# Reordering the plan in front of the first scan: port marks, weight casts and bias rows in a conv-attention hybrid kernel

## The chip, the cores and the metric

The kernel runs on one core of one Trainium2 chip. The metric is the device time of one execution in microseconds, the median of several runs. A core has five engines with queues of their own: PE (TensorE, matrix products into PSUM), DVE (VectorE), ACT (ScalarE), POOL (GpSimd) and SP (SyncE, which here only issues DMAs). Each engine takes its instructions strictly in the order in which the program emitted them. An instruction waits on semaphores for its data only; where two engines share no data, nothing on the chip ties them in time.

## The reference, cut to what matters

Two layers run over `x` of shape (4, 64, 64, 96). Only the beginning of the first bears on the change:

```python
x = x + _L0_conv_ref(_gn(x), ...)      # _gn: group norm, 32 groups of 3 channels, over a whole image
# in _L0_conv_ref:
xn = (x - mu) * rsqrt(var + 1e-3) * ln_gamma + ln_beta       # layer norm over the 96 channels
proj = xn.reshape(B, L, C) @ W_in + b_in                     # L = 4096, 96 -> 3*96 + 3*96*16
# proj is cut into value u, gate, delta d and A, B, C (16 states for each channel)
h_new = d * (A_t * h) + d * (B_t * u_t)                      # a scan along L
y = gate * sum(C_t * h_new, axis=states)
...
# second layer: linear attention, then a feed-forward net in quantised fp8, each with a residual
```

So before the first scan step can run, the group norm of the first image (a mean and a variance over all 4096 positions), the layer norm of the first 512 positions, the transposition and the projections with `W_in` must be done, one after another.

## The kernel before, in words

**Tiling.** Each image of 4096 positions is cut into 8 chunks of 512. For a chunk the scan runs over 12 tiles (`Tile`, L901): 4 groups of states (`sh`) by 3 groups of 32 channels (`cg`), each 128 partitions by 512 positions. There are 384 tiles in all. A tile is three projections on PE (B, A, C, each of three matmuls, L294), ACT's copy of B out of PSUM (`b_copy`, L926), POOL's multiply (`b_mul`, L929), DVE's multiply of A (`a_mul`, L938), the scan on DVE (L945) and a multiply by C (`c_mul`, L969). From the seventh tile (`START = 6`, L1399) on, the main loop (L1588) emits these in a fixed pattern; everything else is hung on steps of that loop.

**Precision.** The projections work in fp32r with a high and a low part. For each weight block ACT casts the high part (`high`, L326), then DVE or POOL subtracts to get the low part (`split_low`, L284), then two SP DMAs build a third, mixed block (`split_copies`, L286 to L288). The blocks are `w_dug` (for d, u and gate), `w_rep` (columns of `w_dug` repeated four times over, written by `repeat`, L316, on ACT; `n = 0` is the high part, `n = 1` the low) and twelve blocks `w_bac[k]` for k = B, A, C and `sh` = 0 to 3. The low parts of `sh` 0 and 1 are DVE's, those of 2 and 3 POOL's. The raw weights come in by SP DMAs at the start, B's first, then A's, then C's.

**The start.** `planned_start` (L1403) lists what has to be done up to the seventh tile as jobs with an engine, a cost, predecessors and a rank. The class `Plan` (L489) is a list scheduler: it takes again and again the job that can start first by its own clock; among jobs within 0.3 us of each other it takes the lower rank, then the longer tail (the cost of all that hangs on the job). Jobs `land(...)` are no instructions: they stand for a time before which something isn't expected. A job marked `port=True` on DVE isn't placed before the last marked job on POOL has ended, and the other way round. The result is only an **order of emission** on each engine; the planner's times do not exist on the chip. Where PE would idle in the plan, filler matmuls (`stay_awake`, L1535) are emitted.

The chain it places first, with the lines of the trace: group norm statistics (L644), aggregate (L647), group means (`m`: L685, L693 to L701), group variances (`r`: L685, L705, and the root on POOL, L708); for each of the two a diagonal on ACT (L719), a `spread` on PE (L725) and `spread_out` on ACT (L734); then for the first chunk `centre` (L780), `scale` (L783), layer norm statistics (L432 to L439), the root on POOL (`rstd`, L410), the apply on DVE (`apply_vector`, L480), transposes (L800), `affine` (L804), `upper` (L808), `low_in_place` (L839, three instructions), the wide products for d and u (L844), `wide_d` on ACT (L849), `wide_du` on DVE (L856), and then the tiles. Beside it lie: `high_dug` and `low_dug`, `repeat`, the bias rows (`bias_rows`, L336 and L340, on DVE; `bias_turn`, L348 and L351, on PE; `bias_out`, L355 and L356, on DVE), the weight casts, and the second chunk's front (`second`: `centre` and `scale` on POOL, statistics on DVE, root on POOL, apply on ACT, transposes, `low`, L813, with three SP DMAs, L814 to L816, and its own d and u). Late weights are loaded by SP in one job (`load_late`, L266).

Of the kernel before, what the change touches and what calls it, by code (L numbers as in the profile page):

```python
# [75 lines left out]
GN_FIRST = (10, 14, 21, 26, 34, 41, 46, 54)  # L76
GN_CHAIN = (0, 0, 1, 2, 6, 6, 8, 8, 8, 9, 11, 11)
XBUFS = 15
END_TRIES = 250
END_SEED = 25  # L80

# [2 lines left out]
def conv_attn_hybrid_kernel(  # L84
# [19 lines left out]
    nc = tc.nc  # L104
# [1298 lines left out]
    def planned_start():  # L1403
        plan = Plan({"A": 2, "B": 1, "C": 1, "D": 1, "M": 3, "bu": 5, "h": 3})
        plan.LOOK = 0.3
        job = plan.job
        plan.rank = -5

        def land(what, time):
            return job(what, time, lambda: None)  # L1410

        def mm(cost, fn, *args, after, key):
            return job("PE", cost, fn, *args, after=after, take=[key])

        q, first, second = GroupNorm(0), Front(0, 0), Front(0, 1)
        x = [land(f"x{n}", 3.6 + 0.8 * n) for n in range(NCH)]
        raw = [land(f"raw{n}", t) for n, t in enumerate((15.8, 19.8, 24.0))]
        a = []
        for n in range(NCH):
            key = f"{'AM'[n % 2]}:g{n}"  # L1420
            t = mm(0.5, q.turn, n, "AM"[n % 2], after=[x[n]], key=key)
            a = [job("DVE", 0.85, q.stats, n, after=[t, *a], free=[key])]
        b = job("DVE", 0.8, bias_rows, after=[x[3]])
        b = mm(0.8, bias_turn, after=[b], key="M:b")
        b = job("DVE", 0.35, bias_out, after=[b], free=["M:b"])
        a = job("DVE", 0.4, q.aggregate, after=a)
        m = job("DVE", 1.1, q.all_of, ("group_sums", "m"), ("mean",), ("squares",), after=[a])
        r = job("DVE", 0.7, q.all_of, ("group_sums", "v"), ("offset",), ("root",), after=[m], late=0.9)
        g = []
        for n, a in enumerate((m, r)):  # L1430
            a = job("ACT", 0.37, q.diagonal, n, n + 1, after=[a, *g])
            a = mm(0.75, q.spread, n, n + 1, after=[a], key=f"M:s{n}")
            g = [job("ACT", 0.25, q.spread_out, n, n + 1, after=[a], free=[f"M:s{n}"])]
            if n == 0:
                c = job("DVE", 0.56, first.centre, nc.vector, after=g)


        calm = land("calm", 22)
        hd = job("ACT", 0.43, high_dug, after=[land("raw", 11.9)])
        ld = job("POOL", 0.8, low_dug, after=[hd])  # L1440
        wd = job("SP", 1.0, split_copies, w_dug[:, 0], w_dug[:, 1], w_dug[:, 2], after=[ld], late=2.2)
        wr = [job("ACT", 0.45, repeat, n, k, after=[(hd, ld)[n]]) for n in range(2) for k in range(2)]
        w = {"rep": job("SP", 1.0, split_copies, *(w_rep[:, n] for n in range(3)), after=wr, late=2.2)}
        for sh in range(NSH):
            plan.rank = 3 * sh - 3
            for k in range(3):
                t = job("ACT", 0.83, high, k, sh, after=[raw[k]])
                if sh < 2:
                    t = job("DVE", 0.8, low, k, sh, nc.vector, after=[t])
                else:  # L1450
                    plan.rank = 1 if k == 0 else 3 * sh - 3
                    t = job("POOL", 1.3, low, k, sh, nc.gpsimd, after=[t, calm])
                    low_b = t if k == 0 else low_b
                v = w_bac[k][:, :, :, sh * P : (sh + 1) * P]
                w[k, sh] = job("SP", 1.0, split_copies, *(v[:, n] for n in range(3)), after=[t], late=2.4)
        plan.rank = -4


        a = job("DVE", 0.56, first.scale, nc.vector, after=[c, *g])
        a = job("DVE", 1.2, first.stats, False, after=[a])  # L1460
        a = job("POOL", 1.05, first.ln.rstd, False, after=[a])
        a = job("DVE", 1.3, lambda: first.ln.apply_vector(first.t, first.t), after=[a])
        a = mm(0.5, first.transpose, after=[a], key="M:x")
        a = job("ACT", 0.74, first.affine, after=[a])
        a = job("ACT", 0.58, first.upper, after=[a])
        for n in range(3):
            a = job("DVE", 0.7, first.low_in_place, n, after=[a], free=["M:x"] if n == 2 else [])
        d, u = [], []
        for cg in range(NCG):
            plan.rank = cg - 4  # L1470
            t = mm(0.7, first.wide, 0, cg, after=[a, w["rep"]], key=f"M:d{cg}")
            d.append(job("ACT", 0.69, first.wide_d, cg, after=[t, b, *d[-1:]], free=[f"M:d{cg}"]))
            t = mm(0.7, first.wide, 1, cg, after=[t], key=f"M:u{cg}")
            u.append(job("DVE", 0.74, first.wide_du, cg, after=[t, d[-1]], free=[f"M:u{cg}"]))


        last = [None] * 3
        s, on_pool = None, {}
        for k in range(START + 3):
            n, (sh, cg) = tiles[k], divmod(k, NCG)  # L1480
            plan.rank = k - 3
            last[0] = t = mm(0.7, n.b_proj, after=[a, w[0, sh], last[0]], key=f"B:{k}")
            t = job("ACT", 0.69, n.b_copy, after=[t], take=[f"bu:{k}"], free=[f"B:{k}"])
            plan.rank = k - 2
            if k < START + 2:
                bu = job("POOL", 1.3, n.b_mul, after=[t, u[cg]])
            plan.rank = k - 2
            if k < START + 1:
                last[1] = t = mm(0.7, n.a_proj, after=[a, w[1, sh], last[1]], key=f"A:{k}")
                t = job("DVE", 0.75, n.a_mul, after=[t, d[cg]])  # L1490
            plan.rank = k
            if k < START:
                s = job("DVE", 1.25, n.scan, after=[t, bu, s], take=[f"h:{k}"],
                        free=[f"A:{k}", f"bu:{k}"])
                c = f"{'CD'[k % 2]}:{k}"
                last[2] = t = mm(0.7, n.c_proj, after=[a, w[2, sh], last[2]], key=c)
                if n.on_pool:
                    t = job("ACT", 0.69, n.c_copy, after=[t, low_b if k == NCG else None], free=[c])
                    if k < START - 1:
                        job("POOL", 1.3, n.c_mul_pool, after=[t, s], free=[f"h:{k}"])  # L1500
                else:
                    job("DVE", 0.75, n.c_mul, after=[t, s], free=[c, f"h:{k}"])
                if k < START - 1:
                    job("ACT", 0.2, n.keep, after=[s])


        plan.rank = 1
        a = job("POOL", 1.0, second.centre, nc.gpsimd, after=[*g, calm])
        a = job("POOL", 1.0, second.scale, nc.gpsimd, after=[a])
        a = job("DVE", 1.2, second.stats, after=[a])  # L1510
        a = job("POOL", 1.4, second.ln.rstd, after=[a])
        a = job("ACT", 1.55, second.apply, after=[a])

        plan.rank = 2
        a = mm(0.5, second.transpose, after=[a, land("then", 38)], key="M:x2")
        a = job("ACT", 0.74, second.affine, after=[a])
        a = job("ACT", 0.58, second.upper, after=[a])
        b = job("DVE", 0.7, second.low, after=[a], free=["M:x2"], late=2.9)
        plan.rank = 5
        a = mm(0.7, first.proj, 1, after=[u[-1], wd], key="M:gate")  # L1520
        job("ACT", 0.68, first.gate_out, after=[a], free=["M:gate"])
        plan.rank = 2
        a = mm(0.7, second.proj, 2, after=[b], key="M:d2")
        a = job("ACT", 0.69, second.d_out, after=[a], free=["M:d2"])
        b = mm(0.7, second.proj, 0, after=[a], key="M:u2")
        a = job("DVE", 0.74, second.du_out, after=[a, b], free=["M:u2"])
        for q in range(4):
            a = job("SP", 1.5, second.spread, q, after=[a])
        plan.rank = 6
        job("SP", 0.5, load_gx, 1, 0, after=[land("free0", 34.0)])  # L1530
        job("SP", 4.0, load_late, after=[land("free1", 37.0)])

        awake = []

        def stay_awake():  # L1535

            if first.ln.r is None or hasattr(tiles[1], "c_ps"):
                return
            if not awake:
                awake.append(bank("D", [P, TC], "awake0"))  # L1540
            nc.tensor.matmul(
                awake[0][:, 0:P], lhsT=ident, rhs=ident, start=True, stop=True
            )

        plan.run(stay_awake)
        return second
# [8 lines left out]
    for b in range(B):  # L1555
        for i in range(NCH):
            g = b * NCH + i
# [101 lines left out]
```

## Time and profile before

| | us |
|---|---|
| median of 3 runs (lowest to highest) | 1138.74 (1137.71 to 1138.97) |
| the profiled execution, its own time | 1137.66 |
| its span, first to last instruction | 1135.9 |

| engine | busy us | share of the span |
|---|---|---|
| PE | 1097.0 | 97% |
| DVE | 1088.2 | 96% |
| POOL | 1029.3 | 91% |
| ACT | 904.8 | 80% |

The time outside the span (1.8 us) lies before the first and after the last instruction. In the stretch in front of the first scan the engines are less full:

| stretch, us | PE | DVE | ACT | POOL | granted PE clock |
|---|---|---|---|---|---|
| 10 to 20 | 5.95 | 6.82 | 5.22 | 1.66 | 0.60 |
| 20 to 30 | 8.37 | 9.73 | 6.91 | 7.28 | 0.72 |
| 30 to 40 | 9.49 | 9.58 | 7.02 | 6.96 | 1.00 |

The first scan begins at 35.51 us. How to read such a table: an engine's busy time includes what an instruction spends waiting after it has begun[...]. So a full engine isn't always a working one, and the mean duration of a line has to be held against the same line elsewhere.

### The profile page before, as it was taken

The numbers are of one execution on the slowest core, as the hardware profiler recorded it, in microseconds if no ns is written. First come the engines' busy times: TensorE is split into PE (matmuls) and PEld (weight loads), VectorE is DVE, ScalarE is ACT, GpSimd is POOL, SyncE is SP. The second block draws the span as 40 slices with busy tenths as digits, with TensorE's granted clock in tenths as the row PEclk, the third lists the DMA queues.
The fourth block names the chain that finished last, engine by engine and source line by source line (L and its number), as shares of the span: only waits on it lengthen the run. The fifth ranks groups of instructions, "written<-read, shape, count | busy, mean of one in ns | idle before, by whom it ended". The sixth has DMA issues, their size and how long they took to land. (4 is left out here: it accounts for less than half of the span.)

```text
span 1135.9 us, 20132 instructions
## 1 busy us (share of the span) xinstructions
PE 1097.0 (97%) x5691; PEld 862.4 (76%) x5691; DVE 1088.2 (96%) x1870; ACT 904.8 (80%) x2452; POOL 1029.3 (91%) x1048
## 2 busy tenths in 40 slices
PE   6999999999999999999999999999999999999985
PEld 5677777877877777777777777777877777777663
DVE  6999999999999999999999999999999999999985
ACT  4577667766766988988898889889888888886577
POOL 5688999999999999999999999999999999999654
PEclk7999999999999999999999999999999999999999
DMA  7578888888888988888888888888898888897432
GB/s 184 129 155 167 189 177 166 186 187 174 182 188 170 189 176 184 180 175 187 182 185 190 187 179 184 173 173 187 176 184 179 168 184 183 171 185 164 91 92 56
DMA packets 98073, 193.61 MB, mean 170 GB/s; under 512 B 48509, under 2 KB 56641, under 8 KB 97962
## 3 DMA queue, kind: packets, MB, share of 16 engines
q0 software_dynamic: 17376, 91.63, 44.6%
q1 hardware_dynamic: 79996, 100.69, 35.6%
q8 instruction: 45, 0.74, 0.3%
q14 instruction: 66, 0.54, 0.1%
q10 hardware_dynamic: 590, 0.02, 0.0%
HBM read 20.36 MB, written 12.58 MB: 29 GB/s over the span
## 5 line engine op out<-in xcount | busy, mean ns | idle before, releaser
L929 POOL TENSOR_TENSOR bu<-bu,rep 128x512 f32<-128x512 f32 x384 | 597.5, 1591 | 13.9 <-ACT bu L926 6.5
L945 DVE TENSOR_TENSOR_SCAN h<-Aps,state,bu 128x512 f32<-128x512 f32 x336 | 427.1, 1271 | 5.5 <-POOL bu L929 1.4
L926 ACT ACTIVATE bu<-Bps,b_bac 128x512 f32<-128x512 f32 x384 | 262.4, 683 | 111.3 <-PE Bps L294 104.8
L938 DVE SCALAR_TENSOR_TENSOR Aps<-Aps,b_bac,rep 128x512 f32<-128x512 f32 x384 | 281.6, 734 | 4.5 <-PE Aps L294 4.2
L294 PE MATMUL Bps<-xs,w 128*128 128x512 f32 x768 | 265.9, 427 | 6.7 <-ACT bu L926 6.5
L294 PE MATMUL Aps<-xs,w 128*128 128x512 f32 x768 | 242.7, 397 | 0.7 <-DVE h L945 0.6
L294 PEld LDWEIGHTS Aps<-xs,w 128*128 128x128 f32 x768 | 142.7, 188 | 39.2 <-DVE h L945 5.9
L978 POOL TENSOR_TENSOR ch<-ch,h 128x512 f32<-128x512 f32 x94 | 151.9, 1616 | 3.9 <-ACT ch L975 3.9
L294 PEld LDWEIGHTS Bps<-xs,w 128*128 128x128 f32 x768 | 128.8, 190 | 30.4 <-ACT bu L926 13.7
L294 PE MATMUL Aps<-xl,w 128*128 128x512 f32 x384 | 151.6, 395 | 0.0
L294 PE MATMUL Bps<-xl,w 128*128 128x512 f32 x384 | 151.5, 394 | 0.0
L294 PE MATMUL Cps<-xs,w 128*128 128x512 f32 x384 | 120.6, 395 | 0.0
L294 PE MATMUL Dps<-xs,w 128*128 128x512 f32 x384 | 120.6, 395 | 0.0
L969 DVE SCALAR_TENSOR_TENSOR ch<-Dps,b_bac,h 128x512 f32<-128x512 f32 x161 | 119.3, 741 | 0.4 <-PE Dps L294 0.3
L985 POOL DMA_DIRECT2D ch<-ch x94 | 107.4, 1142 | 8.6 <-DMA ch<-ch 4.5
L969 DVE SCALAR_TENSOR_TENSOR ch<-Cps,b_bac,h 128x512 f32<-128x512 f32 x129 | 95.5, 740 | 0.0
L294 PEld LDWEIGHTS Bps<-xl,w 128*128 128x128 f32 x384 | 72.2, 188 | 17.7
L294 PEld LDWEIGHTS Aps<-xl,w 128*128 128x128 f32 x384 | 72.0, 188 | 17.7
L294 PEld LDWEIGHTS Cps<-xs,w 128*128 128x128 f32 x384 | 72.0, 188 | 17.5
L294 PEld LDWEIGHTS Dps<-xs,w 128*128 128x128 f32 x384 | 72.0, 187 | 17.6
L294 PE MATMUL Dps<-xl,w 128*128 128x512 f32 x192 | 75.7, 394 | 0.0
L294 PE MATMUL Cps<-xl,w 128*128 128x512 f32 x192 | 75.7, 394 | 0.0
(212 smaller groups left out, 2181.6 us busy)
## 6 DMA issues: line engine op xcount, KB each, us to landing
ch<-ch POOLq DMA_DIRECT2D x94, 768.0 KB, 6.7
rep<-dd SPq DMA_DIRECT2D x372, 128.0 KB, 3.7
ch<-ch POOLq DMA_DIRECT2D x30, 384.0 KB, 5.4
xl<-lo SPq DMA_DIRECT2D x62, 128.0 KB, 3.2
x<-in_x_dram SPq DMA_DIRECT2D x32, 192.0 KB, 3.3
xatd<-xat SPq DMA_DIRECT2D x32, 192.0 KB, 2.8
xal<-xatd SPq DMA_DIRECT2D x32, 192.0 KB, 4.1
out_dram<-o SPq DMA_DIRECT2D x32, 192.0 KB, 3.2
```

The source lines that it names most:

```text
L294: nc.tensor.matmul(ps, lhsT=wt[:, n], rhs=mv, start=(n == 0), stop=(n == 2))
L926: nc.scalar.activation(self.bu, self.b_ps, AF.Identity, bias=self.bias(0))
L929: nc.gpsimd.tensor_tensor(self.bu, self.bu, rep[self.b, self.i][:, self.cg, 1], ALU.mult)
L938: nc.vector.scalar_tensor_tensor(self.a_ps, self.a_ps, self.bias(1), rep[self.b, self.i][:, self.cg, 0], ALU.add, ALU.mult,)
L945: nc.vector.tensor_tensor_scan(self.h, self.a_ps, self.bu, 0.0 if self.i == 0 else state[self.sh, self.cg], ALU.mult, ALU.add,)
L969: nc.vector.scalar_tensor_tensor(self.slot(), self.c_ps, self.bias(2), self.h, ALU.add, ALU.mult)
L978: nc.gpsimd.tensor_tensor(self.ch, self.ch, self.h, ALU.mult)
L985: nc.gpsimd.dma_start(chs[g, base(g)], chs.pop((g, sh)), accum_op=ALU.add)
```

## The change

The plan of the start is given other predecessors, ranks and marks; no instruction is added or removed, and the main loop is left as it is.

- `repeat(1, k)`, the low parts of `w_rep`, now come after the second `spread_out` (`*g`), with rank -3.5.
- The bias rows come after `scale` of the first chunk (`scaled`), with rank -3, where they had rank -5 and only waited for the fourth load of `x`.
- The high casts of the weights come after the second `spread_out`.
- The job `calm` (a fixed 22 us of the planner's clock, before which POOL's casts and the second chunk's `centre` weren't placed) goes. In its place these jobs come after the first chunk's apply (`applied`).
- `port=True` is put on the first chunk's `centre`, `scale` and apply, on `low_dug`, on all low casts, on the first tiles' `b_mul`, and on the second chunk's `centre` and `scale`. The planned cost of the apply is 1.2 instead of 1.3.

```diff
+REPEAT_RANK = -3.5
+BIAS_RANK = -3
...
-        b = job("DVE", 0.8, bias_rows, after=[x[3]])
-        b = mm(0.8, bias_turn, after=[b], key="M:b")
-        b = job("DVE", 0.35, bias_out, after=[b], free=["M:b"])
...
-                c = job("DVE", 0.56, first.centre, nc.vector, after=g)
-        calm = land("calm", 22)
+                c = job("DVE", 0.56, first.centre, nc.vector, after=g, port=True)
         hd = job("ACT", 0.43, high_dug, after=[land("raw", 11.9)])
-        ld = job("POOL", 0.8, low_dug, after=[hd])
+        ld = job("POOL", 0.8, low_dug, after=[hd], port=True)
         wd = job("SP", 1.0, split_copies, w_dug[:, 0], w_dug[:, 1], w_dug[:, 2], after=[ld], late=2.2)
-        wr = [job("ACT", 0.45, repeat, n, k, after=[(hd, ld)[n]]) for n in range(2) for k in range(2)]
+        wr = [job("ACT", 0.45, repeat, 0, k, after=[hd]) for k in range(2)]
+        plan.rank = -4
+        a = job("DVE", 0.56, first.scale, nc.vector, after=[c, *g], port=True)
+        scaled = a
+        a = job("DVE", 1.2, first.stats, False, after=[a])
+        a = job("POOL", 1.05, first.ln.rstd, False, after=[a])
+        a = job("DVE", 1.2, lambda: first.ln.apply_vector(first.t, first.t), after=[a], port=True)
+        applied = a
+        plan.rank = REPEAT_RANK
+        wr += [job("ACT", 0.45, repeat, 1, k, after=[ld, *g]) for k in range(2)]
+        plan.rank = BIAS_RANK
+        b = job("DVE", 0.8, bias_rows, after=[x[3], scaled])
+        b = mm(0.8, bias_turn, after=[b], key="M:b")
+        b = job("DVE", 0.35, bias_out, after=[b], free=["M:b"])
         w = {"rep": job("SP", 1.0, split_copies, *(w_rep[:, n] for n in range(3)), after=wr, late=2.2)}
         for sh in range(NSH):
             plan.rank = 3 * sh - 3
             for k in range(3):
-                t = job("ACT", 0.83, high, k, sh, after=[raw[k]])
+                t = job("ACT", 0.83, high, k, sh, after=[raw[k], *g])
                 if sh < 2:
-                    t = job("DVE", 0.8, low, k, sh, nc.vector, after=[t])
+                    t = job("DVE", 0.8, low, k, sh, nc.vector, after=[t], port=True)
                 else:
                     plan.rank = 1 if k == 0 else 3 * sh - 3
-                    t = job("POOL", 1.3, low, k, sh, nc.gpsimd, after=[t, calm])
+                    t = job("POOL", 1.3, low, k, sh, nc.gpsimd, after=[t, applied], port=True)
...
         plan.rank = -4
-        a = job("DVE", 0.56, first.scale, nc.vector, after=[c, *g])
-        a = job("DVE", 1.2, first.stats, False, after=[a])
-        a = job("POOL", 1.05, first.ln.rstd, False, after=[a])
-        a = job("DVE", 1.3, lambda: first.ln.apply_vector(first.t, first.t), after=[a])
         a = mm(0.5, first.transpose, after=[a], key="M:x")
...
-                bu = job("POOL", 1.3, n.b_mul, after=[t, u[cg]])
+                bu = job("POOL", 1.3, n.b_mul, after=[t, u[cg]], port=True)
...
-        a = job("POOL", 1.0, second.centre, nc.gpsimd, after=[*g, calm])
-        a = job("POOL", 1.0, second.scale, nc.gpsimd, after=[a])
+        a = job("POOL", 1.0, second.centre, nc.gpsimd, after=[applied], port=True)
+        a = job("POOL", 1.0, second.scale, nc.gpsimd, after=[a], port=True)
```

## The prediction

> **What bounds it now.** First the busy time by stages: from 30 to 50 us PE and DVE are each over 94% busy, and over the span 97% and 96%. What the front of the kernel loses is not won back later, and what it gains stays. So I read the 20 us ahead of the first scan, engine by engine, from the timeline (columns: start, us, engine, line, op, out<-in, count, idle time before and who ended it).
>
> ACT carries the group norm's chain:
>
> ```profile
> 16.07 0.51 ACT L318 CAST w_rep<-w_dug 128x384 fp32r<-128x384 f32 x1 [2.12 <-POOL w_dug L284]
> 16.48 0.23 ACT L734 COPY gmr<-gmr_ps 128x96 f32<-128x96 f32 x1
> 16.61 0.37 ACT L719 ACTIVATE gdg<-ident,gm 96x96 f32<-96x96 f32 x1
> 17.82 0.24 ACT L734 COPY gmr<-gmr_ps 128x96 f32<-128x96 f32 x1 [0.43 <-PE gmr_ps L725]
> ```
>
> The first spread's product was ready at 14.7 and its copy-out (L734) ran at 16.48, because `repeat` (L318) stood before it in ACT's queue and waited for the low part of `w_dug` from POOL. Next, POOL and DVE side by side:
>
> ```profile
> 14.39 0.88 POOL L708 TENSOR_TENSOR gm<-gv,mhalf 96x1 f32<-96x1 f32 x1 [5.95 <-DVE gv L705]
> 15.25 0.78 POOL L284 TENSOR_TENSOR w_dug<-raw,w_dug 128x288 fp32r<-128x288 f32 x1
> 19.98 1.52 POOL L410 TENSOR_TENSOR rstd_c<-rstd_c,mhalf 128x4 f32<-128x4 f32 x1 [3.95 <-DVE rstd_c L439]
> 21.45 1.02 POOL L780 TENSOR_TENSOR z<-x,gmr 128x384 f32<-128x384 f32 x1
> 22.55 1.08 POOL L783 TENSOR_TENSOR z<-z,gmr 128x384 f32<-128x384 f32 x1
> 23.60 2.31 POOL L284 TENSOR_TENSOR w<-raw,w 128x384 fp32r<-128x384 f32 x2
> ```
>
> ```profile
> 14.77 1.34 DVE L340 COPY bias<-brow 6x128 f32<-6x128 f32 x1
> 18.09 0.56 DVE L783 TENSOR_TENSOR z<-z,gmr 128x384 f32<-128x384 f32 x1 [0.61 <-ACT gmr L734]
> 19.84 1.52 DVE L284 TENSOR_TENSOR w<-raw,w 128x384 fp32r<-128x384 f32 x2
> 21.53 3.30 DVE L480 TENSOR_SCALAR z<-z,mv_c,rstd_c 128x96 f32<-128x96 f32 x4 [0.17 <-POOL rstd_c L410]
> 24.76 2.47 DVE L284 TENSOR_TENSOR w<-raw,w 128x384 fp32r<-128x384 f32 x2
> 27.25 0.69 DVE L839 TENSOR_TENSOR xs<-xnt_ps,xs 32x512 fp32r<-32x512 f32 x1
> 29.39 2.46 DVE L284 TENSOR_TENSOR w<-raw,w 128x384 fp32r<-128x384 f32 x2
> 33.29 1.41 DVE L856 SCALAR_TENSOR_TENSOR rep<-wide_ps,b_rep,rep 128x512 f32<-128x512 f32 x2 [0.25 <-issue]
> 35.51 1.22 DVE L945 TENSOR_TENSOR_SCAN h<-Aps,bu 128x512 f32<-128x512 f32 x1
> ```
>
> L480 (the layer norm's apply) takes 3.30 us here. The same four instructions in the chain that ended last take
>
> ```profile
> 1084.32 0.96 DVE xn L480 x4
> ```
>
> so 2.3 us is waiting. The instruction begun at 21.53 ends at 22.54, just behind POOL's L780 (22.47); the others end just behind L783 and the first L284. Two DVE casts (L284) take 1.52 us alone and 2.47 beside POOL. Last, PE:
>
> ```profile
> 17.57 5.10 PE L1541 MATMUL awake<-ident 128*128 128x128 f32 x24
> 28.00 1.22 PE L294 MATMUL wide_ps<-xs,w_rep 128*128 128x512 f32 x2
> 29.41 0.50 PE L294 MATMUL wide_ps<-xl,w_rep 128*128 128x512 f32 x1 [0.20 <-DVE xl L839]
> ```
>
> From 29.41 to the seventh scan (53.7) PE has hardly 2 us of gaps, while DVE came to L856 only at 33.29 though its input was ready at 30.7. PE's own start is therefore what the later stretch inherits.
>
> **What the Trainium skill says.** "SBUF — State Buffer", section "Who interferes with whom": a DVE instruction in a two-port mode, or with two SBUF inputs, and a GpSimd instruction that reads SBUF exclude each other; the later one fully blocks. The trace agrees: 3.30 against 0.96, and each end within 0.1 us of POOL's. "VectorE: DVE Perf Modes", section "The perf-mode tier table": fp32 `tensor_scalar` in SBUF has a two-port mode, an operand in PSUM has none; so L839, L856, L938 and the scan are free of it, and none of them is stretched here. "TensorE: Matmul & The Clock Gate", section "Part 1": the clock halves after an idle window of about 3.4 us. The trace grants 0.5 from 12.0 to 22.3 and from 25.7 to 29.1.
>
> **The change, part by part.** Planner times below serve for the order alone; durations are the trace's.
>
> *1. `repeat(1,*)` behind the second spread_out.* ACT's next is then spread_out 0 at 14.75 and the diagonal as soon as the root is there (15.27): 15.32 instead of 16.61. The path behind keeps its length, so `scale` starts at 16.8, **1.3 us earlier**. Both repeats (0.5 each) follow, and the second `w_rep` copy on SP goes out near 17.7 instead of 17.41. It landed at 23.95 behind the last weights' load (22.6 by its semaphore), and is needed near 27: nothing. `centre` (DVE) now meets the root and `low_dug` on POOL from 15.0 and ends near 16.4, still before 16.8: nothing, but with 0.4 us of cover.
>
> *2. Bias rows behind `scaled`.* L336 (0.58), L340 (1.34, some 0.2 if not blocked), five transposes and two copies (0.34) leave 14.26 to 17.5, where the chain no longer meets them. By the ranks and tails DVE has next: stats, the cast `low 0,0`, bias rows, apply. The root (L410) needs 1.01 undisturbed (35.44) and took 1.52 beside two casts. Now it starts at 18.65 beside one cast (to 19.3): it ends between 19.66 and 20.2 (the cast's end plus 0.85). I take 19.9 against 21.50: **1.6 earlier**. The bias product is wanted by `wide_d` after 28: hidden.
>
> *3. `calm` out, `applied` and ports in.* These are the planner's edges, not waits on the chip. After the root POOL's next is by tail (22.8 against 8.8) still the second front's `centre`, then `scale`, then `low 0,2`, whose inputs are there by 16.7 and 19.9. So it starts at the root's end, as at 21.45 now, beside the apply. I leave the apply its 3.3 us plus 0.1 for L340 in front of it: it ends at 23.3 to 23.9, taken 23.4 against 24.84, **1.4 earlier**. Bounds: 0.96 if POOL stood off (2.3 more gained), 3.6 if L340 takes one more blocked turn.
>
> No semaphore is added. What stands longer in a queue is the copy of `w_rep` on SP (ahead of all weight copies, 0.3 us), and bias rows on DVE ahead of the apply, which would wait for the root anyway. The port marks on the multiply (L929) and the POOL casts move only places in the order.
>
> *4. Casts regrouped.* Behind the apply come `low 1,0`, bias_out, `low 0,1`: 0.8+0.3+0.8, with no POOL cast beside them, since POOL's next (`low 1,2`) waits for an ACT cast behind `upper`. They end at 25.3, as `upper` does. Today the casts there took 2.47 and kept L839 from 26.7 to 27.25. So L839 runs 25.3 to 27.4: **2.0 earlier**. ACT's `high` casts began at 17.95 anyway; behind g they begin at 17.4: nothing.
>
> *5. PE.* The fillers are laid by planned gaps: 9 (of two matmuls) instead of 8 stand before the wide products and end near 27.2; at half clock the first product then ends 28.1 to 28.6 instead of 29.91. I take **1.6 earlier**.
>
> *6. DVE to the first scan.* Two casts instead of two casts, stretched, plus statistics stand before L856: it starts near 29.0, the multiply (L929) near 30.2, the scan near 32.5, 3.0 earlier. But `low 2,1` (0.8 us on DVE) and two more POOL casts (2.4 us) then still lie behind it, and PE has gained only 1.6. PE's stalls that came of a late DVE (0.13 at 34.0, half of 0.47 at 39.0) may go: 0.3.
>
> **Sum**: 1.6+0.3 = 1.9 us off the profiled execution's 1137.66 (span 1135.9 and 1.8 around it). It stands 1.1 below the median 1138.74, so I forecast 1138.74-1.9 = **1136.8**. Own range: 1135.7 (all of the scan's 3.0) to 1137.7 (1.0, where the half clock lasts).
>
> **Rivals.** *The plan holds on the chip*: POOL stays off the apply. It ends 2.3 us sooner and the gain is 4.2: 1134.5. For it: the plan says so. Against: at 21.45 POOL did not wait for the plan's time either, and no data ties the two. *Taken back by the clock*: transposes ragged over 21 to 24 leave PE no busy window, and it runs at half for one window more: 3.4 us at half is 1.7 lost, 1138.5. For it: 25.7 to 29.1 now. Against: the fillers behind. *SP's queue, slower*: with today's order four POOL casts are done at 31.2; in mine two, and four with two SP copies each (0.59) lie ahead of the second front's `low` copies. Those start at 45.20 now, the moment `lo` is ready, and PE takes them at 48.7 with no slack. POOL has six multiplies (1.29), a root (1.2) and four casts (1.18) from 30.2: done at 43.9, with blocked turns (1.50 at 29.73) 45.5. It decides from 43.9 on: with a copy behind it 46.8, with the late weights' 4.0 us of issues too 50.8, that is 1.6 to 5.6 later than now. With some PE gap taken up I put it at +2.8: 1141.5.
>
> **Numbers.** Mine 0.43, plan holds 0.22, clock 0.18, SP 0.17. A measurement can tell about 0.2%, 2.3 us. Faster by that: over a third of mine (0.16) and nearly all of the second, 0.37; slower: most of the last, 0.15; within: 0.48. The range 1133.9 to 1141.2 leaves out the edges of the second and the last.
>
> **What would show it.** After: spread_out 0 near 14.8 and `scale` near 16.8 (step 1); L410 ending near 19.9 (2); L780 on POOL starting at L410's end and L480 at 3.3 us (3; an L480 near 1.0 means the first rival); L839 at 25.3 (4); the first `wide` ended by 28.6, clock 1.0 by 29.1 (5); the scan near 32.5 (6). Wrong if SP's L814 lies later than 45.2, or PE waits there.

## The result, and the profile after

| | kernel before | changed kernel |
|---|---|---|
| median, 21 runs each | 1138.74 us | 1136.67 us |
| ratio, 95% interval | | 0.9982 (0.9976 to 0.9988) |
| the profiled execution, its own time | 1137.66 | 1135.46 |
| its span | 1135.9 | 1133.7 |

The change makes the kernel 2.1 us faster (1.4 to 2.7 by the interval); 1.9 had been forecast. In the changed file the lines shown here stand two further down (L480 is L482, L839 is L841). One thing must be known before two traces are compared here: the group norm waits for `x` from memory and for PE, and its root (the first POOL line of the stretch) begins at 14.39 us in the profiled execution before and at 14.16 after. That 0.23 us is not the change's: two executions of one and the same later version (e4 and g1 below) have their roots at 14.46 and 14.13. Below, "behind the root" means counted from the root's beginning.

ACT, from the timeline (start, us, engine, line, operation, tiles, count, idle time before and who ended it):

```profile
14.50 0.24 ACT L736 COPY gmr<-gmr_ps 128x96 f32<-128x96 f32 x1 [0.78 <-PE gmr_ps L727]
...
15.96 0.24 ACT L736 COPY gmr<-gmr_ps 128x96 f32<-128x96 f32 x1 [0.83 <-PE gmr_ps L727]
16.09 0.93 ACT L320 CAST w_rep<-w_dug 128x384 fp32r<-128x384 f32 x2
```

The copy-out now runs as soon as PE has the product (it waited for PE, not for a cast), and both `repeat` casts follow the second copy-out. POOL:

```profile
18.12 1.51 POOL L412 TENSOR_TENSOR rstd_c<-rstd_c,mhalf 128x4 f32<-128x4 f32 x1 [2.64 <-DVE rstd_c L441]
19.59 1.02 POOL L782 TENSOR_TENSOR z<-x,gmr 128x384 f32<-128x384 f32 x1
```

The second chunk's `centre` (L782) starts the moment the layer norm's root (L412) ends. The mark that was to keep it off the apply does nothing here. DVE shows the consequence:

```profile
16.23 0.56 DVE L785 TENSOR_TENSOR z<-z,gmr 128x384 f32<-128x384 f32 x1 [0.33 <-ACT gmr L736]
...
19.67 3.30 DVE L482 TENSOR_SCALAR z<-z,mv_c,rstd_c 128x96 f32<-128x96 f32 x4 [0.25 <-POOL rstd_c L412]
...
24.82 0.69 DVE L841 TENSOR_TENSOR xs<-xnt_ps,xs 32x512 fp32r<-32x512 f32 x1 [0.25 <-ACT xs L810]
...
30.17 1.01 DVE L441 TENSOR_SCALAR rstd_c<-mv_c 128x4 f32<-128x4 f32 x1
...
32.68 1.22 DVE L947 TENSOR_TENSOR_SCAN h<-Aps,bu 128x512 f32<-128x512 f32 x1
```

The apply takes 3.30 us as before. `low_in_place` now waits for ACT instead of standing behind stretched casts. And PE:

```profile
26.39 1.04 PE L296 MATMUL wide_ps<-xs,w_rep 128*128 128x512 f32 x2
27.27 0.40 PE L296 MATMUL wide_ps<-xl,w_rep 128*128 128x512 f32 x1
```

The first wide product ends at 27.67 instead of 29.91. The 48th scan comes 2.49 us earlier behind the root, and that distance holds within 0.03 us from the 11th to the 108th tile, so that the 48th scan is a fair gauge of what the start has gained. From there to the end it wanders; more on that below.

### The profile page after: what moved, and what is told of

Read it like the earlier page. It is cut to its first block, busy times and chain, and to the rows that moved or that the text cites. A ratio compares the mean times of both kernels' runs of the same rounds, so it can differ in the third digit from the quotient of the medians.

```text
span 1133.7 us, 20116 instructions
## 1 busy us (share of the span) xinstructions
PE 1095.7 (97%) x5687; PEld 862.9 (76%) x5687; DVE 1087.2 (96%) x1870; ACT 905.1 (80%) x2452; POOL 1028.4 (91%) x1048
```

## The experiments

Kernels whose names in the table share a letter (e, f, g) ran on one chip, with the kernel before beside them. The table is the summary. "First wide" is the end of the first wide product and "48th scan" the start of that scan, both behind the root, as a difference to the kernel before in one profiled execution each. The ratio is that of the times, with its 95% interval. Two executions of one program differ in the two middle columns by 0.6 us (changed and f1) or hardly at all (e4 and g1), so a smaller difference than that is not read from them.

| kernel | first wide, us | 48th scan, us | ratio of times |
|---|---|---|---|
| changed | -2.01 | -2.49 | 0.9982 (0.9976 to 0.9988) |
| changed, again (f1) | -1.37 | -1.88 | 0.9981 (0.9971 to 0.9990) |
| before, `repeat` moved alone (e1) | -1.23 | -2.38 | 0.9978 (0.9966 to 0.9990) |
| before, bias rows moved alone (e2) | -0.15 | +0.13 | 0.9996 (0.9988 to 1.0005) |
| changed, `repeat` put back (f2) | -0.16 | +0.16 | 1.0017 (1.0005 to 1.0030) |
| changed, port marks of the front out (e3) | -1.61 | -1.09 | 0.9974 (0.9965 to 0.9983) |
| changed, POOL held off the apply (e4) | -3.98 | -4.06 | 0.9960 (0.9946 to 0.9974) |
| the same again (g1) | -3.98 | -4.09 | 0.9957 (0.9945 to 0.9970) |
| before, POOL held (g3) | -2.81 | -1.56 | 0.9991 (0.9982 to 1.0000) |
| changed, no second fillers (f3) | -1.76 | -0.98 | 0.9969 (0.9957 to 0.9980) |
| held longer, POOL's casts late (f4) | -4.45 | +1.19 | 0.9997 (0.9987 to 1.0007) |
| the same, last copies ahead of the spreads (g2) | -4.45 | -5.30 | 0.9949 (0.9936 to 0.9961) |

### One part alone, and one part undone

The kernel before with the `repeat` moved and nothing else:

```diff
-        wr = [job("ACT", 0.45, repeat, n, k, after=[(hd, ld)[n]]) for n in range(2) for k in range(2)]
+        wr = [job("ACT", 0.45, repeat, 0, k, after=[hd]) for k in range(2)]
+        plan.rank = -3.5
+        wr += [job("ACT", 0.45, repeat, 1, k, after=[ld, *g]) for k in range(2)]
+        plan.rank = -5
```

> The kernel before with one part alone: the two low repeats come after the second spread_out. My theory: the copy-out of the first spread runs near 14.8 instead of 16.5 and scale near 16.8, 1.3 us earlier; all behind keeps its shape (two casts beside the root, apply 3.3 us), so the first scan is 1.3 earlier and the time 1.0 to 1.3 us shorter, some 1137.5. Rival (the chain was held by the bias rows and casts, not by repeat): under 0.4 us gained.

Its time is 0.9978 (0.9966 to 0.9990) of the kernel before: all that the whole change brings, and rather more than the 1.0 to 1.3 us expected (2.5 us, 1.1 to 3.9). Yet the chain gained less than the 1.3 us of step 1, because behind the first instruction that held it up stood a second. PE's timeline in this kernel:

```profile
15.71 0.27 PE L351 MATMUL bias_ps<-ident,bias 6*128 6x6 f32 x1 [0.86 <-DVE bias L340]
15.90 0.74 PE L725 MATMUL gmr_ps<-gdg,ones 96*128 96x96 f32 x2
```

The bias rows' last transpose waits for DVE's blocked copy (L340, 1.34 us), and the second `spread` (L725) waits behind it in PE's queue. `scale` starts 3.02 us behind the root, against 3.70 before and 2.07 in the changed kernel. The rest of this kernel's gain shows on DVE. First DVE, then POOL:

```profile
23.63 1.52 DVE L284 TENSOR_TENSOR w<-raw,w 128x384 fp32r<-128x384 f32 x2
...
27.70 1.57 DVE L284 TENSOR_TENSOR w<-raw,w 128x384 fp32r<-128x384 f32 x2
```

```profile
26.36 1.19 POOL L284 TENSOR_TENSOR w<-raw,w 128x384 fp32r<-128x384 f32 x1 [2.71 <-ACT w L326]
28.64 1.65 POOL L284 TENSOR_TENSOR w<-raw,w 128x384 fp32r<-128x384 f32 x1 [1.08 <-ACT w L326]
```

The two pairs of casts take 1.52 and 1.57 us where they took 2.47 and 2.46 before. ACT, in the kernel before and here:

```profile
17.95 4.58 ACT L326 CAST w<-raw 128x384 fp32r<-128x384 f32 x6
```

```profile
17.64 3.83 ACT L326 CAST w<-raw 128x384 fp32r<-128x384 f32 x5
```

In front of `affine` ACT makes five weight casts here instead of six; so POOL's second cast waits 2.71 us for its input and stays off DVE's first pair. In the second pair it is POOL's cast that waits: it begins at 28.64, behind the second of DVE's (28.45 to 29.27), and takes 1.65 us. Moving the `repeat` thus did two things. The expectation named the first; the second is step 4 of the forecast, which didn't say that it hangs on the `repeat`. The granted clock is a third difference: it stays full from 22.0 on here, and was at half from 25.7 to 29.1 before, so a part of the gain may be the clock's.

The bias rows alone:

```diff
-        b = job("DVE", 0.8, bias_rows, after=[x[3]])
...
+        plan.rank = -3
+        b = job("DVE", 0.8, bias_rows, after=[x[3], a])
```

> The kernel before with one part alone: bias rows after scale, at rank -3. My theory: scale stays near 18.1, because repeat still holds ACT; the bias rows take the place of one of the two casts in front of the apply, and a third cast comes to stand in front of wide_du; the time stays within 0.6 us of before. Rival (bias rows on DVE held the chain): scale 0.6 or more earlier and the time 1 us or more shorter.

Nothing measurable, as expected: 0.9996 (0.9988 to 1.0005). `scale` comes 0.33 us earlier behind the root, because the root itself takes 0.55 us without the bias copies beside it, 0.88 with them. The first scan is later, not earlier, since three DVE casts stand in front of `wide_du`.

The other way round, the changed kernel with the `repeat` put back:

```diff
-        wr = [job("ACT", 0.45, repeat, 0, k, after=[hd]) for k in range(2)]
+        wr = [job("ACT", 0.45, repeat, n, k, after=[(hd, ld)[n]]) for n in range(2) for k in range(2)]
...
-        plan.rank = REPEAT_RANK
-        wr += [job("ACT", 0.45, repeat, 1, k, after=[ld, *g]) for k in range(2)]
```

> The changed kernel with one part undone: repeat(1, 0) and repeat(1, 1) stand again where they stood, in front of the first and the second spread_out on ACT. Theory (the copies of the low part held the group norm's chain, and this is the one link by which the change gains): scale starts 3.3 to 3.5 us after the group norm's root begins, instead of 2.1; the first wide product and the first scan come about 1.2 us later than in the changed kernel; the time lies 0.8 to 1.6 us above it. Rival (the parts overlap: bias rows alone brought 0.3 us, repeat alone nearly all, since each alone relieves the same chain): with the bias rows gone the repeat matters less, the time is within 0.4 us of the changed kernel. A second rival (everything beside the repeat is worth nothing, as the bias rows alone were): the time goes back to the kernel before, 1.9 to 2.2 us above the changed kernel.

1.0017 (1.0005 to 1.0030): slower than the kernel before and 4.1 us above the changed kernel beside it, so that the second rival of this expectation is nearest and even it falls short. ACT in this kernel:

```profile
15.77 0.51 ACT L320 CAST w_rep<-w_dug 128x384 fp32r<-128x384 f32 x1 [1.64 <-POOL w_dug L286]
16.19 0.23 ACT L736 COPY gmr<-gmr_ps 128x96 f32<-128x96 f32 x1
```

The old picture is back, and the first wide product ends 0.16 us earlier than before where the changed kernel has 1.4 to 2.0. All other parts together bring the front nothing without the `repeat`. Why the time is 0.17% longer while the 48th scan lies only 0.16 us later is not settled. In its profiled execution 1.7 us are lost in the last 90 us. Of these, 1.0 falls in a stretch with PE's clock at half (1117.4 to 1124.2), which was at full in the kernel before; whether the other executions have it too isn't known.

### The port marks

The changed kernel without nine marks of the start:

```diff
-                c = job("DVE", 0.56, first.centre, nc.vector, after=g, port=True)
+                c = job("DVE", 0.56, first.centre, nc.vector, after=g)
...
-                    t = job("POOL", 1.3, low, k, sh, nc.gpsimd, after=[t, applied], port=True)
+                    t = job("POOL", 1.3, low, k, sh, nc.gpsimd, after=[t, applied])
```

> The changed kernel with all port marks of the start taken off (the edges and ranks of the change kept). My theory: the marks only move places in the order. POOL stands beside the apply either way (3.3 us); a third cast on DVE stands in front of wide_du and POOL does four casts before its first multiply; the first scan comes 0.8 to 1.6 us later than with the marks, and the time lies 0.3 to 1.0 us above the changed kernel's, still 1 us or more under before. Rival (the marks keep the two engines apart and bring the gain): apply longer than 3.3 us and the time back at before's.

The apply takes 3.30 us again: the marks have no part in it, in either direction. Their effect lies in the order behind it:

```profile
26.89 3.20 DVE L286 TENSOR_TENSOR w<-raw,w 128x384 fp32r<-128x384 f32 x3
```

Without marks three casts stand in front of `wide_du`, which starts at 30.01, 15.96 us behind the root instead of 14.30, and the 48th scan is 0.8 to 1.4 us later than in the changed kernel's two executions. (PE's clock was at half up to 28.9 in this one, up to 27.1 and 27.7 in those, so a part of it can be the clock's.) The time, expected 0.3 to 1.0 us above the changed kernel's, doesn't show that loss: 0.9974 (0.9965 to 0.9983) here, 0.9982 (0.9976 to 0.9988) there, and the intervals overlap.

### POOL really held off the apply

What the marks mean to do, done with data: POOL copies one column of what the apply writes last, in front of the second chunk's `centre` and of its own weight casts.

```diff
+        kept = job("POOL", 0.1, lambda: nc.gpsimd.tensor_copy(junk[:, 0:1], first.t[:, J - 1, C - 1 : C]), after=[applied])
...
-        a = job("POOL", 1.0, second.centre, nc.gpsimd, after=[applied], port=True)
+        a = job("POOL", 1.0, second.centre, nc.gpsimd, after=[kept], port=True)
```

> The changed kernel with one more instruction on POOL, in front of the second front's centre: a copy of one element of the apply's last output, so that POOL really waits for the apply. My theory: the apply takes near 1.0 us instead of 3.3, low_in_place starts 2.3 us earlier (near 22.5), the first scan near 30.5, and the time is 1.2 to 2.3 us below the changed kernel's, near 1134.8. Rival (other things are late then: w_rep lands near 24, the C weights near 22.6, POOL's work runs into its first multiplies): the wide products start no earlier than 26, and the time is within 0.5 us of the changed kernel's.

DVE, then POOL's copy:

```profile
19.98 1.05 DVE L482 TENSOR_SCALAR z<-z,mv_c,rstd_c 128x96 f32<-128x96 f32 x4 [0.27 <-POOL rstd_c L412]
...
21.84 1.48 DVE L286 TENSOR_TENSOR w<-raw,w 128x384 fp32r<-128x384 f32 x1
...
25.48 2.32 DVE L286 TENSOR_TENSOR w<-raw,w 128x384 fp32r<-128x384 f32 x2
```

```profile
21.09 0.66 POOL L1449 COPY junk<-z 128x1 f32<-128x1 f32 x1 [1.15 <-DVE z L482]
```

Now the apply takes 1.05 us. So its 2.3 us were POOL's, as the fit of the ends had suggested. The section on the chip says that nothing ties two engines in time that share no data. That holds for when an instruction begins: in the changed kernel POOL's `centre` didn't wait for the apply. It doesn't hold for how long one takes: the two share no data, and the apply took 3.30 us beside it. The transposes come together, PE's clock stays full from 20.3 on, and the 48th scan lies 4.06 us before the kernel before. The time is 0.9960 (0.9946 to 0.9974). It ran once more, beside two others:

> The held version of the earlier run once more (the changed kernel with POOL's copy of one column of the first chunk's z in front of the second chunk's centre), as the measure for the two beside it: apply about 1.05 us, first wide product near 26.0, the 48th scan 4.0 us earlier than in the kernel before. If what is gained in front is kept, the time is 3.0 to 4.2 us under the kernel before (ratio 0.9963 to 0.9974); if later stretches take part of it, as they did in its profiled execution (2.0 us at the 198th to 214th tile), 2.0 to 3.0 us under it, not to be told from the changed kernel.

0.9957 (0.9945 to 0.9970), 4.9 us. The gain in front is kept. The collision hasn't gone altogether: POOL's `centre` now meets one of DVE's casts (1.48 us), and two of POOL's casts, from 24.09 to 26.44, meet the next two (2.32 us).

The hold alone, in the kernel before (POOL's casts wait for the copy here too):

```diff
+        kept = job("POOL", 0.1, lambda: nc.gpsimd.tensor_copy(junk[:, 0:1], first.t[:, J - 1, C - 1 : C]), after=[a])
...
-        a = job("POOL", 1.0, second.centre, nc.gpsimd, after=[*g, calm])
+        a = job("POOL", 1.0, second.centre, nc.gpsimd, after=[*g, calm, kept])
```

> The kernel before with the hold alone: POOL copies one column of the first chunk's z, which only the apply writes last, in front of the second chunk's centre and its own casts; nothing of the change is in it, and repeat and bias rows stand where they stood. Theory (POOL's blocking of the apply is a cost of its own, beside the repeat's hold on the chain): the apply takes 1.0 us and ends at 22.6 instead of 24.84, low_in_place starts 1.4 to 2.2 us earlier, the first wide product ends 1.2 to 2.0 us earlier, and the time is 1.0 to 2.0 us under the kernel before. Rival (the repeat is the one link that counts: with the chain late, PE's half clock and DVE's casts beside POOL's four hold the start): the time is within 0.5 us of the kernel before.

The apply is short and the first wide product 2.81 us earlier, more than expected. Then DVE becomes the bound (DVE, POOL and PE):

```profile
26.31 2.92 DVE L284 TENSOR_TENSOR w<-raw,w 128x384 fp32r<-128x384 f32 x2
```

```profile
22.38 1.37 POOL L1465 COPY junk<-z 128x1 f32<-128x1 f32 x1 [1.15 <-DVE z L480]
...
25.76 5.70 POOL L284 TENSOR_TENSOR w<-raw,w 128x384 fp32r<-128x384 f32 x4
```

```profile
32.20 0.73 PE L294 MATMUL wide_ps<-xs,w_rep 128*128 128x512 f32 x2 [1.19 <-DVE rep L856]
```

Four POOL casts in a row fall on DVE's two and on its statistics, and PE waits 1.19 us for `wide_du`. Of 2.81 us, 1.56 are left at the 48th scan; the time is 0.9991 (0.9982 to 1.0000), 1.0 us at the middle, which doesn't decide between the two expectations. The held version of the changed kernel has two POOL casts there, not four, and a chain that is 1.2 us shorter to begin with; it kept all it had won.

### PE's clock

The changed kernel once more, beside three variants:

> The changed kernel once more, as the measure for the three runs beside it. Expected at the kernel before's median less 2.1 us (ratio 0.9976 to 0.9988, as measured for it), with the apply at 3.3 us in four blocked pieces and the half clock over one window of 3.4 us between 20 and 28 us. If the held apply of the earlier run is really worth 1.3 us on top, this run must lie 1 to 2 us above that one's distance to the kernel before (which was -4.0).

0.9981 (0.9971 to 0.9990): the ratio repeats, and e4's lies 2.4 us further, where 1 to 2 had been expected. The clock doesn't repeat. The stretch from 20 to 26 us (its length; busy time and instructions of PE, its weight loads, DVE, ACT and POOL; the granted clock; the DMA share and GB/s), in the first execution:

```profile
20.00:26.00 6.00, 4.18 (x25) 3.69 (x25) 5.72 (x10) 3.26 (x5) 3.20 (x4) 0.78 0.78 169
```

and in this one:

```profile
20.00:26.00 6.00, 4.50 (x21) 3.79 (x21) 5.57 (x10) 3.74 (x6) 3.07 (x4) 0.50 0.72 165
```

It is the same program. In one execution the clock rose at 20.3 and fell at 23.7, in the other it stayed at half from 14.0 to 27.7. The first wide product ends 0.64 us later there, the 48th scan 0.61. PE isn't idle in front of that product: it is still at work on the fillers, which at half clock last longer. Now without the fillers between the transposes and the first wide product:

```diff
-            if first.ln.r is None or hasattr(tiles[1], "c_ps"):
+            if first.ln.r is None or hasattr(first, "ps"):
```

> The changed kernel without the nine pairs of filler matmuls between the transposes and the first wide product; no other instruction differs. It prices the clock, step 5. If a window at half clock costs what I put on it (three wide products and what follows at 0.63 instead of 0.39 us a matmul): PE is idle from 23.3 to 25.5, the granted clock stays at 0.5 for one window more, to about 30.5, some 14 matmuls run at half, 0.2 us more each; the first wide product itself isn't later (its third matmul waits for the third low_in_place, 26.9), the fourth to the sixth product are, and the time is 1.0 to 2.0 us above the changed kernel. Rival: DVE sets the pace there (its casts end at 28.5 and stand in front of wide_du), so that PE's slower products are covered: within 0.4 us of the changed kernel.

PE in this kernel:

```profile
27.73 1.05 PE L296 MATMUL wide_ps<-xs,w_rep 128*128 128x512 f32 x2
...
31.57 0.66 PE L296 MATMUL wide_ps<-xs,w_rep 128*128 128x512 f32 x2
```

The front behaves as expected: half clock until 31.6, pairs of matmuls at 1.05 us instead of 0.63, the 48th scan 0.90 us later than in the changed kernel beside it (1.51 later than in its first execution). The first wide product itself ends 0.4 us earlier than in the execution beside it, since no fillers stand in front of it. The time doesn't follow: 0.9969 (0.9957 to 0.9980), if anything below the changed kernel's, where 1.0 to 2.0 us above it had been expected. The clock moves in steps of 3.4 us. This kernel was at half for one step more than f1 and two more than the changed kernel's first execution, and f1 for one more than that first one. So a step at half clock goes with 0.6 to 0.9 us at the 48th scan, and whether that reaches the end isn't shown.

### SP's queue

Held longer: the copy on POOL reads the low part that DVE writes behind the apply, and POOL's casts come after the first `b_mul`.

```diff
+                    if (k, sh) == (0, 1):
+                        low_01 = w_bac[0][:, 1, NCG - 1, 2 * P - 1 : 2 * P].bitcast(F32)
+                        kept = job("POOL", 0.1, lambda: nc.gpsimd.tensor_copy(junk[:, 0:1], low_01), after=[applied, t])
...
+                if k == 0:
+                    for t in lows:
+                        t["after"].append(bu)
```

> The changed kernel with POOL held back longer: a copy of one column on POOL reads the low part that DVE writes behind the apply (low 0,1), and stands in front of the second chunk's centre; and POOL's weight casts come behind the first b_mul. So POOL meets neither the apply nor DVE's casts at 21 to 27 us. In the held run DVE's casts still took 1.48 and 2.32 us for 0.8 and 1.6. Expected if these collisions lie on the path: low_in_place starts at the end of upper (0.5 us earlier than in the held run), the first wide product ends near 25.5 instead of 26.0, wide_du starts 0.4 to 1.1 us earlier, and the time is 0.3 to 1.0 us below the held run, so 1.6 to 3.0 us below the changed kernel. Rival: POOL's casts are only put off and fall between the first tiles' multiplies, where they make b_mul late: then the first scan is earlier, the sixth to tenth are not, and the time equals the held run's or lies up to 1 us above it.

In front it does what it should: first wide product -4.45 us, the eighth to tenth scan 4.6 us early. Then 5.8 us are lost in three tiles, and the time is that of the kernel before, 0.9997 (0.9987 to 1.0007), where a gain of 1.6 to 3.0 us over the changed kernel had been expected. PE's longest wait between 44 and 66 us (waited for, total, times, longest), and SP's queue:

```profile
PE Dps L296 <- DMA w<-w: 3.4, 1, 3.4
```

```profile
47.48 7.55 SPq L866 DMA_DIRECT2D rep<-dd  x12
...
55.83 1.59 SPq L290 DMA_DIRECT2D w<-w  x1
```

The copies of the last weight block (C, `sh` = 3) are issued from 55.07 on, behind twelve spreads of 7.55 us in all, and PE stands before the first product that needs it. That is 3.4 of the 5.8 us; the rest goes in the next two tiles, while PE's clock is at half from 61.6 to 68.4. One edge more:

```diff
-            a = job("SP", 1.5, second.spread, q, after=[a])
+            a = job("SP", 1.5, second.spread, q, after=[a, *w.values()])
```

> The version held longer, with POOL's casts behind the first b_mul, and one thing more: on SP the last weights' copies (C, sh = 3) stand in front of the twelve DMAs that spread d and u of the second chunk, instead of behind them. In that version the first ten scans came 4.6 us early and then PE waited 3.8 us for that copy, issued at 55.8 behind 7.6 us of spreads. Theory (SP's queue was the cause, the prediction's last rival in another place): the copy is issued near 48, PE doesn't wait at the tenth to twelfth tile, the 48th scan lies 4.3 to 4.7 us before the kernel before, and the time is 0.3 to 1.0 us under the held version. Rival (POOL's late casts are the cause by themselves, done only at 47.2): PE waits all the same, the 48th scan is 0 to 2 us early. A second rival: the spreads, begun 1.2 us later, hold the second chunk's first tiles: the gain is lost at the thirteenth tile.

SP's queue in this kernel:

```profile
47.94 0.59 SPq L290 DMA_DIRECT2D w<-w  x1
48.63 9.44 SPq L866 DMA_DIRECT2D rep<-dd  x12
```

PE doesn't wait for the copy, the clock stays full, the 48th scan lies 5.30 us before the kernel before, and the time is 0.9949 (0.9936 to 0.9961). That is clearly below the changed kernel; against the held version (0.9957 and 0.9960) the intervals overlap. The two programs differ in this edge alone, so the order on SP was worth the whole difference between f4 and g2.

## Why the prediction was right, step by step

The likeliest case came true: the size (1.9 forecast, 2.1 measured), its first reason (the `repeat`, as e1 and f2 show), and what was to tell it from its rival, POOL starting under the apply. Each step, with the 0.23 us of the earlier root added to what was measured so that it compares with the forecast:

1. **`repeat`.** Copy-out forecast 14.8, measured 14.73; `scale` forecast 16.8, measured 16.46. The extra 0.34 is the root: 0.55 us instead of 0.88, because the bias copies no longer run beside it. Step 2 of the forecast counted the bias rows' relief on the second root only. `centre` ended at 16.12 with 0.34 of cover: it met `low_dug` (1.12 us instead of 0.56), hidden as forecast. The step missed that the bias rows also held the second `spread` on PE; alone, the `repeat` gives the chain 0.68. That the step came out is luck in this respect: the change moves both.
2. **Root of the layer norm.** Forecast to end at 19.9, measured 19.86; it began 0.3 earlier than forecast and lost that again: it took 1.51 us beside the one cast and the two bias copies that follow it.
3. **Apply.** Forecast 3.3 us with POOL starting at the root's end; measured 3.30 and so. The held version gives the bound of 2.3 us named there its proof.
4. **Casts.** `low_in_place` forecast 25.3, measured 25.05; both pairs of casts unstretched (1.58 for two), as forecast and for the reason given: POOL's second cast waited 2.72 us for ACT.
5. **PE.** Forecast 1.6 us, measured 2.01 in one execution and 1.37 in the other. The step reckoned with half clock and an end at 28.1 to 28.6; the second execution, at half clock, ends at 28.5 so counted, the first, with a step of full clock from 20.3, at 27.9. The mechanism stands; that the clock can stand differently in the same program the step didn't have.
6. **DVE to the first scan.** Forecast 3.0 us, measured 2.60 (1.96 in the other execution). The statistics' L441 took 1.01 instead of 0.17 us beside POOL's `b_mul`: a collision that the step overlooked. As it said, this distance isn't what stays: the 48th scan moved by 2.49 and 1.88, near the first wide product's 2.01 and 1.37 and 0.5 more. So the stalls of PE that go were worth 0.5, not 0.3.

What the sum didn't say: at `scale` the parts don't add. The `repeat` alone brings it 0.68 us earlier, the bias rows alone 0.33, the change 1.63, because either one stands ready behind the other. At the 48th scan this is no longer seen: the `repeat` alone gives -2.38, the rest alone +0.16, both -2.49 and -1.88. So the `repeat` is nearly all of the change; bias rows, ranks and marks change where the same gain is taken.

The rivals: the plan didn't hold on the chip (3.30 us). The clock did take 0.6 back in one of two executions, a third of what its case reckoned. SP's queue was not slower: L816 starts at 42.61 (45.20 before), and PE waited 0.2 us for `lo`. But f4 shows the same mechanism in another place: once POOL's casts end late, there at 47.2, their copies stand behind other DMAs. Its price, 5.8 us, lies a little above the 1.6 to 5.6 that the rival named; but the DMAs in front are others, and a part of it is the clock's.

What stays open is the later part. From the 108th tile on the distance to the kernel before wanders by 1 to 3 us (in e1's by 5 up to the end), in another way in each execution, and differently for the same program. PE's waits between 575 and 612 us in one held execution:

```profile
PE o_ps L1052 <- POOL yg L1047: 1.0, 1, 1.0
PE gk_ps L1156 <- POOL gram L1094: 0.8, 1, 0.8
```

In the changed kernel's first execution the second of these is 0.3 us and the first isn't there. So POOL's results are there sometimes a little too late for PE. What decides it was not tried. One piece can be read at the end: the profiled executions of e1, e2 and f2, and no others, had PE's clock at half for two steps from 1117 to 1124, and each of the three loses 1.0 us there against the kernel before. All this may be why e3, f3 and f2 stand some 2 us (f4 1.5) off the line that the others form between the 48th scan and the time.

## What to carry to other kernels

In a start that is one chain, look for what stands in front of the chain in each queue, and look again after the first holder is gone: here a cast on ACT hid a transpose on PE. An edge in a scheduler's plan ties two engines only if there is data behind it; a copy of one column was enough, and it took the gain from 2.1 and 2.2 us to 4.6 and 4.9. Before a transfer's source is moved late, walk its queue to the end: twelve short DMAs in front of one weight block's copies took back 5.8 us, with what the clock added, and one edge gave them back.

## What the runs showed of the hardware

- The granted clock changes in steps of 3.41 us (13.46, 20.29, 23.70, 27.11 in one execution of the changed kernel; 14.04 and 27.7, four steps on, in the other), and the steps lie differently in each execution. In the first 36 us of the 13 traces it rose from half to full after 18 steps, in which PE was busy for 90 to 100% of the time, and stayed at half after 18 others, with PE busy for 29 to 89%.
- The prediction took it that the clock halves after an idle step. Less was enough here: it fell after 18 steps in which PE was still 26 to 58% busy, in the kernel before after 22.25 to 25.66 with 58% and no gap over 0.82 us. But it stayed full after steps with 53% and more, in e1's from 22.03 to 28.86 with 63 and 67% and gaps of up to 0.83 us. So a gap doesn't decide it, and the busy share alone not quite; what does was not tried by itself.
- POOL's own instructions are stretched too: the copy of one column took 0.18 us free, 0.66 beside one DVE cast and 1.37 beside two. So the wait that protects DVE costs POOL more than its plan says.
- POOL's root of 96 values took 0.88 us beside DVE's bias copies and 0.55 without them.
